# A bias product moved ahead of the first products, and v's bias loaded as columns, in an attention kernel

## The chip, the cores and the metric

The kernel runs on one core of one Trainium2 chip. The metric is the device time of one launch in microseconds. Times here are medians of several runs of the same program; the profile is of one further execution.

## The reference

The inputs are x of shape (4, 64, 64, 256), three weight matrices with their biases, and a factor gamma, all in float32. Each of the four images is self-attention over its 4096 positions:

```
q = x @ Wq + bq            # (B, 64, 64, 128)
k = x @ Wk + bk            # (B, 64, 64, 128)
v = x @ Wv + bv            # (B, 64, 64, 256)
pq, pk, pv = (t.reshape(B, -1, 4096) for t in (q, k, v))
energy = einsum('bcn,bcm->bnm', pq, pk)
attention = softmax(energy, axis=-1)
out = einsum('bcm,bnm->bcn', pv, attention)
return gamma * out.reshape(B, 64, 64, 256) + x
```

## The kernel before

Each product in float32 is made of three products of a shorter type (`F32R`), so every operand is first split into three forms: `h`, an upper part, `l`, the rest, and `d`, the difference of both. ScalarE (ACT) makes `h` (line 154), VectorE (DVE) makes `l` and `d` (L164); from the third x of the first image on, `two=True`, DVE makes only `l` (L157) and GpSimd (POOL) makes `d` (L160). The products of a group run in the order 2, 0, 1 of the forms: form 2, which is `d`, comes first, in a call of its own, and its result is then scaled in place and gets its bias before forms 0 and 1 are added to it in PSUM.

The order of all instructions is written out by hand (`manual_schedule`): each engine runs its own instructions in the order of the program's text, and waits for others by semaphores. DMAs are issued from the queues of SP (`nc.sync`), ACT (`nc.scalar`) and POOL (`nc.gpsimd`).

The prologue is what the change touches. It loads the weights (`raw`), the biases bq, bk and bv as rows on one partition (`rows`), and the first pieces of x (`xs4`, four slots of 128 x 512 numbers; there are `NI` = 16 pieces to an image). It keeps TensorE (PE) busy with `warm(n)`, n products of a matrix of ones that nobody reads (L139). `weights(0)` and `weights(1)` make the forms of the weights of q and k together and of v: ACT `h` (L173), DVE or POOL a scaled copy (L171), DVE `d` and `l` (L175, L177). These and the forms of x are generators: each `next` emits one step.

For each piece i of x the first image then does:

- `transposed` (L215): four transposes on PE, into one of two PSUM banks; `x_forms` (L154 to L164);
- `products(0, i, 0, (2,))` and `(0, 1)`: q and k, four and eight matmuls (L240), with `seed_qk` between them, in which DVE scales what is there and adds `bias` (L251);
- `qk_forms`: ACT (L269) and DVE twice (L272), and their stores by SP (L293);
- `products(0, i, 1, (2,))` and `(0, 1)`: v, likewise, with `seed_v` between them, in which ACT scales and adds `bvs`, a column for each half (L258 twice); `v_forms`.

The accumulators of these products take turns over four PSUM banks, so the third x's first products need the bank that `qk_forms` of the first x reads.

`bias` has bq and bk on every partition: a product of a row of ones and `rows` spreads them (L591), and ACT scales the result (L592). `bvs` has bv as two columns; two products with one column each turn the row bv (L610), and ACT scales them (L617). Both are made in the prologue and used for all images. `ident`, the identity that the transposes need, is made by POOL, and `gam` is loaded through POOL's queue (L142) and scaled twice (L602, L603).

After the 16 pieces the main loop goes over the images, in each over 8 groups of 512 positions and, for each group, 16 pairs of blocks of 128: energy products (L322, L337), exponentials (L340), their forms and sums on ACT and DVE, and the products with v (L394), with the next image's projections spread among them.

Of the kernel before, what the change touches and what calls it, by code (L numbers as in the profile page):

```python
# [20 lines left out]
def kernel(  # L21
# [36 lines left out]
    nc = tc.nc  # L58
# [42 lines left out]
    with ExitStack() as fast:  # L101
# [22 lines left out]
        nc.scalar.dma_start(raw[:, 0, :, C2:], wk.rearrange("(k p) d -> p k d", p=P))  # L124
        nc.sync.dma_start(raw[:, 1], wv.rearrange("(k p) e -> p k e", p=P))
        nc.gpsimd.memset(zs, 1.0)
        rows = work.tile([P, 2, XB], F32, tag="xin", name="rows", bufs=1)[:1]
        rows = rows.rearrange("p s f -> p (s f)")
        make_identity(nc, ident)
        nc.vector.tensor_scalar(ones_r, zs.to_broadcast([P, P]), 1.0, None, ALU.mult)  # L130
        nc.scalar.dma_start(rows[:, :C2], bq.unsqueeze(0))
        nc.scalar.dma_start(rows[:, C2:C], bk.unsqueeze(0))
        nc.scalar.dma_start(rows[:, C:], bv.unsqueeze(0))
        nc.scalar.activation(zs, zs, AF.Exp)
        wp = ps_e.tile([P, P], F32, tag="e", name="wp")

        def warm(times):
            for _ in range(times):
                nc.tensor.matmul(wp, ones, ones, start=True, stop=True)  # L139
# [70 lines left out]
        def transposed(b, i):  # L210
            xs = loads.pop(("x", b, i))
            tp = units["xt", b, i] = bank(f"xt_{b}_{i}", [P, KC, 2, P], b, 0)
            for k in range(KC):
                for s in range(2):
                    nc.tensor.transpose(tp[:, k, s, :], xs[:, s, k * P : (k + 1) * P], ident)  # L215
# [11 lines left out]
        def products(b, i, w, fs):  # L227

            xf = units["xf", b, i]
            if fs[0] == 2:  # L230
                units[w, b, i] = bank(f"qv{w}_{b}_{i}", [P, 2, C], b, 1)
            to = units[w, b, i]
            for s in range(2):
                for f in fs:
                    for k in range(KC):
                        if w:
                            left, right = wf[:, 1, f, k, s * P : (s + 1) * P], xf[:, f, k]
                        else:
                            left, right = xf[:, f, k, s, :], wf[:, 0, f, k]
                        nc.tensor.matmul(  # L240
                            to[:, s, :],
                            left,
                            right.rearrange("p s a -> p (s a)") if w else right,
                            start=(f == 2 and s == k == 0),
                            stop=(f == 1 and k == KC - 1),
                            skip_group_check=True,
                        )
# [337 lines left out]
        next(x0)  # L585
        next(x0)
        next(w0)
        next(w1)
        products(0, 0, 0, (2,))
        bb = ps_e.tile([P, KC + C], F32, tag="e", name="bb")  # L590
        nc.tensor.matmul(bb[:, KC:], ones[:1], rows[:, :C], start=True, stop=True)  # L591
        nc.scalar.activation(bias, bb[:, KC:], AF.Identity, scale=REST)  # L592
        seed_qk(0, 0)
        transposed(0, 1)
        load_x(0, 4)
        x1 = x_forms(0, 1)
        next(x1)
# [6 lines left out]
        for i in range(NI):  # L604
            products(0, i, 0, (0, 1))
            qk = qk_forms(0, i)
            next(qk)
            if i == 0:
                for eh in range(KC):
                    nc.tensor.matmul(  # L610
                        bb[:, eh : eh + 1],
                        rows[:, C + eh * P : C + (eh + 1) * P],
                        ones[:1, :1],
                        start=True,
                        stop=True,
                    )
                nc.scalar.activation(bvs, bb[:, :KC], AF.Identity, scale=REST / E)  # L617
                products(0, 0, 1, (2,))
                seed_v(0, 0)
                transposed(0, 2)  # L620
                load_x(0, 5)
                x2 = x_forms(0, 2)
                next(x2)
            if i + 1 < NI:
                products(0, i + 1, 0, (2,))
                seed_qk(0, i + 1)
            next(qk)
            next(qk)
            next(qk, None)
            if i == 0:  # L630
                next(x2)
            products(0, i, 1, (0, 1))
            vs = v_forms(0, i)
            next(vs)
            next(vs)
            next(vs, None)
            if i + 1 < NI:
                products(0, i + 1, 1, (2,))
                seed_v(0, i + 1)
            if i + 3 < NI:  # L640
                transposed(0, i + 3)
                for _ in x_forms(0, i + 3):
                    pass
            load_x(0, i + 6)
            store()
            if i in (7, 10):
                cross(i // 9)
            elif i in (8, 11):
                energy(i // 9)
            elif i in (9, 12):  # L650
                upper(i // 10)
            elif i == 14:
                halves(0)
            if 1 <= i <= NJ:
                load_q(0, 0, i - 1)
            if i in (2, 4, 6):
                load_k(i // 2 - 1)
            elif i in (8, 11):
                load_k(3 + i // 9)
# [274 lines left out]
```

## Time and profile before

| what | value |
|---|---|
| time, median of 3 runs | 2359.55 us (2359.01 to 2359.71) |
| profiled execution, its own time | 2358.56 us |
| its span, first to last instruction | 2356.7 us |
| mean granted TensorE clock | 0.997 |
| busy: PE, DVE, ACT, POOL | 2341.8, 2128.1, 1871.1, 389.1 us |
| DMA | 413.69 MB, mean 176 GB/s |

PE, DVE, ACT and POOL are the engines; PEld is PE's weight load, which overlaps its matmuls; SP issues DMAs. A name such as `qv L240` is the tile that is written and the line of the kernel; an arrow in "L251 <- PE qv" names what ended an engine's wait. The profile lists a float32 matmul as several records; a matmul of the shorter type is one. Times within the profile count from its first instruction.

### The profile page before, as it was taken

The page shows a single profiled execution, that of the slowest core. Times are in us where ns is not written, and L with a number is a line of the kernel's source. Part 1 is how long each engine was busy: PE and PEld are TensorE (multiplying, and loading weights), DVE is VectorE, ACT ScalarE, POOL GpSimd, SP SyncE. Part 2 cuts the span into 40 slices and gives each one's busy share as a digit, 9 for nine tenths or more (in the row PEclk, how much of TensorE's full clock was granted, in tenths as well). Part 3 has the DMA queues.
Part 4 walks back from the last instruction along what each step waited for, and adds up shares of the span by engine and source line. Part 5 has one row for each costly group of instructions (what it writes and reads, how often), then busy time and mean ns, then how long its engine had stood idle before and what let it go on. Part 6 is the DMA issues. An engine that isn't in the chain of part 4 may idle for free.

```text
span 2356.7 us, 31990 instructions
## 1 busy us (share of the span) xinstructions
PE 2341.8 (99%) x11110; PEld 1956.9 (83%) x11110; DVE 2128.1 (90%) x2098; ACT 1871.1 (79%) x3075; POOL 389.1 (17%) x665
## 2 busy tenths in 40 slices
PE   9999999999999999999999999999999999999998
PEld 8888888888888888888888888888888888888886
DVE  7989999989999899998999999999989888888888
ACT  6788778888788887888878888778887777888785
POOL 6211111111211111111121111111112111111110
PEclk9999999999999999999999999999999999999999
DMA  8556665556975556555597555665559554444453
GB/s 267 165 162 178 175 175 156 174 150 174 305 241 176 147 174 187 161 159 162 157 344 222 162 165 157 178 173 158 172 152 352 160 134 120 122 130 118 130 130 96
DMA packets 178764, 413.69 MB, mean 176 GB/s; under 512 B 25986, under 2 KB 76421, under 8 KB 178596
## 3 DMA queue, kind: packets, MB, share of 16 engines
q0 software_dynamic: 94144, 280.53, 45.2%
q1 hardware_dynamic: 83902, 130.77, 15.5%
q8 instruction: 91, 1.49, 0.3%
q14 instruction: 77, 0.63, 0.1%
q10 hardware_dynamic: 550, 0.26, 0.0%
HBM read 306.51 MB, written 104.98 MB: 175 GB/s over the span
## 4 chain that ended last, share of the span: by engine, by line
PE 97%; ACT 1%; DVE 1%; issue 0%; DMA 0%; POOL 0%; DVEq 0%; ACTq 0%
PE a L394 39%; PE e L337 20%; PE b L394 19%; PE e L322 10%; PE qv L240 8%; PE xt L215 1%; PE z L432 1%; ACT x L340 0%; ACT o L408 0%; ACT e L323 0%; DVE f L272 0%; DMA xs<-in_x_dram 0%; DVE v L164 0%; ACT h L346 0%; DVE ld L373 0%
## 5 line engine op out<-in xcount | busy, mean ns | idle before, releaser
L340 ACT ACTIVATE x<-e 128x512 f32<-128x512 f32 x960 | 522.3, 596 | 295.5 <-PE e L337 289.2
L357 DVE TENSOR_TENSOR s<-s,x 128x1024 f32<-128x1024 f32 x480 | 587.2, 1223 | 93.4 <-ACT x L340 90.8
L371 DVE TENSOR_TENSOR ld<-x,h 128x1024 fp32r<-128x1024 f32 x480 | 586.8, 1222 | 88.7 <-ACT h L346 57.9
L394 PE MATMUL a<-h,v 128*128 128x512 f32 x2048 | 641.0, 394 | 0.0
L323 ACT ACTIVATE e<-e 128x512 f32<-128x512 f32 x1024 | 546.8, 572 | 108.9 <-PE e L322 108.6
L394 PE MATMUL a<-ld,v 128*128 128x512 f32 x2048 | 632.8, 390 | 0.0
L394 PE MATMUL b<-ld,v 128*128 128x512 f32 x2048 | 631.7, 390 | 0.5 <-DVE ld L373 0.4
L309 POOL DMA_DIRECT2D k<-kf x512 | 272.2, 532 | 1912.2 <-PE e L337 1800.0
L373 DVE SCALAR_TENSOR_TENSOR ld<-h,x 128x1024 fp32r<-128x1024 f32 x480 | 585.5, 1220 | 0.0
L337 PE MATMUL e<-q,k 128*128 128x512 f32 x2048 | 548.9, 390 | 1.1
L346 ACT ACTIVATE h<-x 128x1024 fp32r<-128x1024 f32 x480 | 510.4, 1063 | 13.3
L394 PEld LDWEIGHTS b<-ld,v 128*128 128x128 f32 x2048 | 384.1, 188 | 83.8 <-issue 1.1
L394 PEld LDWEIGHTS a<-ld,v 128*128 128x128 f32 x2048 | 384.4, 188 | 83.1
L337 PEld LDWEIGHTS e<-q,k 128*128 128x128 f32 x2048 | 383.1, 188 | 84.5 <-ACT e L323 6.0
L394 PEld LDWEIGHTS a<-h,v 128*128 128x128 f32 x2048 | 368.6, 189 | 69.4 <-ACT o L408 7.3
L322 PE MATMUL e<-q,k 128*128 128x512 f32 x1024 | 316.0, 390 | 0.0
L322 PEld LDWEIGHTS e<-q,k 128*128 128x128 f32 x1024 | 191.7, 188 | 40.7 <-issue 0.2
L240 PEld LDWEIGHTS qv<-wf,xf 128*128 128x128 f32 x768 | 107.5, 192 | 11.2 <-POOL xf L160 1.1
L240 PE MATMUL qv<-wf,xf 128*128 128x256 f32 x768 | 112.9, 286 | 2.4 <-DVE xf L164 0.9
L240 PEld LDWEIGHTS qv<-xf,wf 128*128 128x128 f32 x768 | 106.7, 192 | 8.4 <-ACT s L433 0.7
L240 PE MATMUL qv<-xf,wf 128*128 128x256 f32 x768 | 110.9, 284 | 0.4 <-ACT s L433 0.3
L272 DVE SCALAR_TENSOR_TENSOR f<-f,qv 128x512 fp32r<-128x512 f32 x128 | 85.9, 682 | 3.4 <-ACT f L269 3.1
(82 smaller groups left out, 1016.5 us busy)
## 6 DMA issues: line engine op xcount, KB each, us to landing
k<-kf POOLq DMA_DIRECT2D x512, 384.0 KB, 3.7
vf<-vf SPq DMA_DIRECT2D x48, 768.0 KB
v<-vf POOLq DMA_DIRECT2D x48, 768.0 KB, 8.1
kf<-f SPq DMA_DIRECT2D x128, 192.0 KB
qd<-f SPq DMA_DIRECT2D x128, 192.0 KB
q<-qd POOLq DMA_DIRECT2D x31, 768.0 KB, 4.7
o<-in_x_dram POOLq DMA_DIRECT2D x31, 512.0 KB, 7.4
out_dram<-o SPq DMA_DIRECT2D x31, 512.0 KB
```

The lines of the kernel that those rows point to most:

```text
L240: nc.tensor.matmul(to[:, s, :], left, right.rearrange("p s a -> p (s a)") if w else right, start=(f == 2 and s == k == 0), stop=(f == 1 an ...
L272: nc.vector.scalar_tensor_tensor(f[:, :, :, j, :], h.bitcast(F32), s, y, ALU.mult, op)
L309: nc.gpsimd.dma_start(t, kf[b, u % NU])
L322: nc.tensor.matmul(e, *forms(n, i, 2), start=True, stop=False, skip_group_check=True)
L323: nc.scalar.mul(e, e, -REST)
L337: nc.tensor.matmul(e, *forms(n, i, f), start=False, stop=(f == 1), skip_group_check=True)
L340: nc.scalar.activation(x[:, i, :], e, AF.Exp, scale=(1.0 + E) ** 3 / E)
L346: nc.scalar.activation(h, units[n], AF.Identity, scale=UPPER)
L357: nc.vector.tensor_tensor(s, s, x, ALU.add)
L371: nc.vector.tensor_tensor(l, x, h.bitcast(F32), ALU.subtract)
L373: nc.vector.scalar_tensor_tensor(d, h.bitcast(F32), 1.0 + E, x, ALU.mult, ALU.subtract)
L394: nc.tensor.matmul(to, vall[:, t, f, i, j * P : (j + 1) * P], units[n][f][:, i, :], start=(t == 0 and i == 0 and f != 1), stop=(t == NU - ...
```

## The change

The change does four things in the prologue.

- The product that spreads bq and bk (L591, now L589) and ACT's scaling of it (L592, now L590) come before `next(w1)` and ahead of the first form-2 products of q and k.
- bv is no longer a part of `rows`. Two DMAs from POOL's queue, issued ahead of the identity, write it straight into the two columns of `bvs`; POOL scales these in place. The two products L610 and ACT's L617 go, and so does the load of bv as a row in ACT's queue.
- One more `warm(1)` follows the transposes of the second x.
- The second step of the third x's forms (`l` on DVE and `d` on POOL) moves from behind `qk_forms` of the first x to right behind the first step.

```diff
         nc.gpsimd.memset(zs, 1.0)
-        rows = work.tile([P, 2, XB], F32, tag="xin", name="rows", bufs=1)[:1]
-        rows = rows.rearrange("p s f -> p (s f)")
+        for eh in range(KC):
+            nc.gpsimd.dma_start(bvs[:, eh : eh + 1], bv[eh * P : (eh + 1) * P].unsqueeze(1))
+        rows = work.tile([P, XB], F32, tag="xin", name="rows", bufs=1)[:1]
         make_identity(nc, ident)
         nc.vector.tensor_scalar(ones_r, zs.to_broadcast([P, P]), 1.0, None, ALU.mult)
         nc.scalar.dma_start(rows[:, :C2], bq.unsqueeze(0))
-        nc.scalar.dma_start(rows[:, C2:C], bk.unsqueeze(0))
-        nc.scalar.dma_start(rows[:, C:], bv.unsqueeze(0))
+        nc.scalar.dma_start(rows[:, C2:], bk.unsqueeze(0))
...
         next(w0)
+        bb = ps_e.tile([P, C], F32, tag="e", name="bb")
+        nc.tensor.matmul(bb, ones[:1], rows, start=True, stop=True)
+        nc.scalar.activation(bias, bb, AF.Identity, scale=REST)
         next(w1)
+        nc.gpsimd.tensor_scalar(bvs, bvs, REST / E, None, ALU.mult)
         products(0, 0, 0, (2,))
-        bb = ps_e.tile([P, KC + C], F32, tag="e", name="bb")
-        nc.tensor.matmul(bb[:, KC:], ones[:1], rows[:, :C], start=True, stop=True)
-        nc.scalar.activation(bias, bb[:, KC:], AF.Identity, scale=REST)
         seed_qk(0, 0)
         transposed(0, 1)
+        warm(1)
         load_x(0, 4)
...
             if i == 0:
-                for eh in range(KC):
-                    nc.tensor.matmul(
-                        bb[:, eh : eh + 1],
-                        rows[:, C + eh * P : C + (eh + 1) * P],
-                        ones[:1, :1],
-                        start=True,
-                        stop=True,
-                    )
-                nc.scalar.activation(bvs, bb[:, :KC], AF.Identity, scale=REST / E)
                 products(0, 0, 1, (2,))
                 seed_v(0, 0)
                 transposed(0, 2)
                 load_x(0, 5)
                 x2 = x_forms(0, 2)
+                next(x2)
                 next(x2)
...
             next(qk, None)
-            if i == 0:
-                next(x2)
             products(0, i, 1, (0, 1))
```

## The prediction

> **What bounds the kernel now.** I read the page first, for what sets the end.
>
> ```profile
> PE 2341.8 (99%) x11110; PEld 1956.9 (83%) x11110; DVE 2128.1 (90%) x2098; ACT 1871.1 (79%) x3075; POOL 389.1 (17%) x665
> ...
> PE 97%; ACT 1%; DVE 1%; issue 0%; DMA 0%; POOL 0%; DVEq 0%; ACTq 0%
> ```
>
> PE is busy for 99% of the span of 2356.7 us and is 97% of the chain that ended last. The change leaves that work alone: it touches only the first 20 us, so all that it can win or lose is there. Next I read the chain in order of time, its beginning:
>
> ```profile
> 7.44 0.64 PE bb L591 x2
> ...
> 8.52 0.71 DVE qv L251
> ...
> 9.28 2.07 PE qv L240 x8
> 11.35 0.94 PE bb L610 x4
> 12.29 1.15 PE qv L240 x4
> 13.44 0.85 PE xt L215 x4
> ...
> 17.75 1.29 POOL xf L160
> ...
> 19.08 2.18 PE qv L240 x16
> ...
> 21.70 2.88 PE qv L240 x24
> ```
>
> Ahead of 19.08 PE alternates with ACT, DVE and POOL: it waits for the bias (ACT's L592 and DVE's L251, 8.10 to 9.28) and for the third x's last form (DVE's L157 and POOL's L160, 17.07 to 19.08). From 19.08 the chain is PE without a gap to about 65 us, in periods of 3.32 us. Last, the table by stretches; after the stretch and its length come the busy times of PE, PEld, DVE, ACT and POOL, then the granted clock:
>
> ```profile
> 5.41:8.83 3.42, 2.40 (x14) 1.50 (x13) 2.68 (x5) 1.67 (x4) 1.91 (x3) 1.00 0.85 286
> 8.83:12.24 3.41, 2.96 (x13) 2.73 (x13) 2.78 (x5) 1.06 (x2) 0.00 (x0) 0.50 0.29 77
> 12.24:15.65 3.41, 3.41 (x17) 3.41 (x17) 0.46 (x1) 1.58 (x4) 0.00 (x0) 0.50 0.00 0
> 15.65:19.07 3.42, 2.59 (x22) 2.38 (x21) 3.31 (x6) 2.43 (x5) 1.32 (x2) 1.00 0.59 201
> ```
>
> ```profile
> 8.00:9.00 1.00, 0.66 (x5) 0.42 (x4) 0.48 (x1) 0.69 (x2) 0.47 (x3) 0.91 0.38 131
> ```
>
> From 8.83 to 15.65 PE runs at half clock: 0.91 over 8 to 9 is half for the last 0.17 us, and the same table has 0.67 for 15 to 16, half for the first 0.65. That is 6.83 us, two stretches of 3.41. A matmul of L240 then takes 0.22 us (0.85 for the four transposes at 13.44) instead of 0.12 (2.88 for 24). PE was 70% busy in the stretch before the clock fell, and 76% in 15.65 to 19.07, after which it stayed.
>
> **The change, part by part.** I follow it to one mark: the start of the first products of the third x, 19.08 now. After it PE is full, so what is won there reaches the end, if DVE keeps up; it does, since in each 3.32 us period its queue waits 0.23 us for ACT (L157 on L154).
>
> *The bias product moved up.* Its rows land at 4.20 and 5.58, and PE is idle from 5.85 to 6.71; the product takes 0.64 and fits there, ending about 6.4. ACT then writes `bias` at 6.4 to 6.8, ahead of its second weight form (L173, 6.49 now), which goes to about 6.7 to 7.3. Behind that stands the second x's first form, due at 7.9: covered. The form's reader, L175 on DVE, needs POOL's `scaled` at 8.06 anyway. L251 now waits only for DVE's own L177, which ends at 7.85, so it runs 7.77 to 8.47 instead of 8.52 to 9.22, and the eight products start at 8.53 instead of 9.28: **0.75 won**. If the rows landed later, the first 0.9 us of that would still cost nothing.
>
> *One warm-up (2 records, 0.22) and the transposes* stand at 7.3 to 8.1, where PE would wait for L251: nothing.
>
> *v's bias by DMA.* The four L610 records and L617 go: 0.94 on PE's path at half clock, **0.94 won** (0.5 at full clock, by half the row). Added are two POOL DMAs and one POOL multiply. The nearest row is the other small POOL load:
>
> ```profile
> 1.49 0.71 POOL L142 DMA_DIRECT2D gam<-in_L_conv_gamma_dram  x1 [0.17 <-issue]
> ```
>
> ```profile
> DMA to landing us min/median/max: 4.8/4.8/4.8
> ```
>
> Two issues at 0.71 push the identity from 1.32 to 2.74; the transposes need it at 4.18, when x lands: 1.4 us of cover. The three loads land at about 5.7, 6.4 and 7.7 by 4.8 each. The multiply (0.22, as L602) stands behind `scaled` on POOL, done at 8.3; ACT needs it at 10.3. Bounds: nothing for a landing up to about 9.9, and one us for each us after that. A gain is excluded, since nothing waits for these but L258. I take nothing, as gam's row has the same number of 4-byte pieces.
>
> *bv's row* leaves ACT's queue (0.28): its table load starts earlier, but ACT then waits for Wk until 4.45 as before: nothing. SP's loads of the third and fourth x go out 0.3 to 0.9 earlier behind Wv in the same queue: nothing, as they are needed at 10 and 12.8.
>
> *The third x's second form moved up.* DVE idles 3.58 us ahead of L251 at 15.19; L157 (0.69) goes into that, and POOL's L160 (1.29) starts behind it instead of after L272. The wait of PE from about 18.1 to 19.08 goes: **about 1.0**. L157 now stands ahead of L251 of the second x and of both L272; L251 ends about 0.2 before PE needs it, so a cost appears only if ACT gives the form more than 0.2 late, at most 0.69. What is late next is L272: the third x's product reuses the bank that L272 reads.
>
> *The clock.* In the changed kernel PE is busy in 5.41 to 8.83 from 5.41 to 6.35, 6.71 to 8.1 and 8.53 to 8.83: 2.63 us, 77%. That is over the 76% that kept the clock and the 70% that lost it. So I take it that the clock is kept. Then, from 8.53: 8 products to 9.58 (0.12 each, 0.1 to start), 4 to 10.05, transposes to 10.49, 4 to 10.96; ACT's two L258 end at 11.18, so PE waits to 11.24 (a new wait of 0.28); 8 and 4 to 12.8, transposes to 13.2, 8 to 14.16; POOL's form is there at 13.8, and L272 ends at 14.19. The mark falls at 14.24 instead of 19.08: **4.84 won**. Of it 0.75 is the bias, 0.94 L610, 1.0 POOL's wait; the rest, 2.1, is the clock net of the new waits. A tenth goes for starts that I didn't see; I take 4.75.
>
> The profiled execution took 2358.56 (span 2356.7 and 1.86 around it), 0.99 under the median of 2359.55. The sum gives 2358.56 - 4.75 = 2353.81, and with that 0.99 **2354.8** for the median.
>
> The clock is where a rule speaks against the change. The Trainium skill, "TensorE: Matmul & The Clock Gate", section "Why this matters for your kernels", asks only that PE has no gap over about 3 us; the longest gap ahead of 8.83 is 0.85 and the clock fell, so the trace differs and the measurement decides.
>
> **The rivals.** *One stretch at half clock.* Counted by matmul time alone (0.12 and 0.11 a record, 0.64 for the bias) the stretch that lost the clock has 2 warm-up records, 4 of L240, the bias and 4 transposes, 1.78 us (52%); in the one that kept it 16 of L240 and 4 transposes begin, 2.36 us (69%); the changed one has 1.78 + 0.22 (warm-up) + 0.30 (from 8.53) = 2.30 (67%): in between. If that is too little, the clock falls at 8.83 and is back at 12.24, PE being full. Then the eight products have some 2.5 records at full clock, and the rest to 12.24 at 0.215: the second x's first products end at 12.5, not 14.95; the mark comes at 15.3, 3.8 won: 2355.75. For it speaks that 87% busy in 8.83 to 12.24 did not bring the clock back.
> The Trainium skill, same page, "Part 4: PE-mode transpose", says transposes don't count as busy in the same way; without their 0.44 the stretches are 39% (lost), 56% (kept) and 54% (changed), the same order, so the trace before can't tell.
>
> *Two stretches at half clock, as before*, if the gate looks at something that the fill doesn't change. Then POOL's wait is hidden either way; PE goes at 0.215 from 8.83 to 15.65 and comes to the mark at 16.8: 2.3 won, 2357.25. Against it: PE would be full from 8.53 on, as in 12.24 to 15.65, which brought it back.
>
> *The gain stops at DVE* between 66 and 75 us, where the chain is DVE's: 2359.5. Against it: DVE's work follows PE's products there and moves with them.
>
> *Slower: v's bias lands late.* ACT's L258 and, on POOL, the third x's form stand behind the landing. If the 4-byte pieces go one by one, at four times gam's 4.8 us, they land at 1.6 + 19.2 = 20.8; L258 ends at 22.0 and the products that follow start there instead of at 14.95; with POOL's wait and the half clock behind that gone, 5.7 are lost: 2365.2. It is slower from a landing of about 15 on. Against it: gam's row.
>
> **How the numbers follow.** Clock kept 0.48; one stretch 0.27; two 0.10; stops at DVE 0.05; late landing 0.05; unforeseen 0.05. 0.2% (4.7 us) is about what a measurement of this kernel can tell from no change; the forecast lies just beyond it. I count three quarters of the forecast's chance and a little of the second case (the runs' half clock can have been longer than the profile's, being 1 us over it) as faster: 0.40. Slower is the late landing and little more: 0.06. The range goes from 2353.7 (kept, and the 0.99 of the median over the profile won too) to 2357.4 (two stretches).
>
> **What would show it.** Right: clock 1.00 in every stretch from 5.41 on; L251's first at 7.8; no L610; no idle PE ahead of the third x's first products, at about 14.3; periods of 3.32 from there. Wrong: 0.50 in any stretch after 8.83 (rivals one and two), a wait of L258 for POOL or a DMA (the slower one), idle PE at L215 before 4.2 grown (identity late), or more idle PE at 66 to 76 than now.

## The result and the profile after

The change took 2354.91 us (median of 22 runs, 2352.77 to 2357.05), the kernel before beside it 2358.92 us (22 runs, 2355.47 to 2360.45): a ratio of 0.9984, 95% interval 0.9978 to 0.9991, so 4.0 us faster by the medians. The forecast was 2354.8. Left out here and below are one run of k_later (2577.58 us) and one of before beside it (2911.9 us), with mean clocks of 0.85 and 0.75. The profiled execution of the change took 2357.05 us (span 2355.3), the longest of its 22, so its first 20 us say more than its total. First the page: PE's busy time, and the shares of the chain that ended last.

```profile
PE 2340.0 (99%) x11108; PEld 1955.6 (83%) x11108; DVE 2127.6 (90%) x2098; ACT 1870.2 (79%) x3074; POOL 391.2 (17%) x668
...
PE 97%; ACT 1%; DVE 1%; issue 1%; DMA 0%; POOL 0%; SPq 0%; ACTq 0%; DVEq 0%; POOLq 0%
```

What bounds the kernel is as before. PE was busy for 2341.8 us then: the 1.8 us less are the two products L610 and the time at half clock, net. The chain of waits in order of time (start, length, what ran) has the prediction's steps one by one:

```profile
6.15 0.64 PE bb L589 x2
...
7.80 0.70 DVE qv L251
...
8.55 1.23 PE qv L240 x8
...
10.80 0.46 ACT qv L258
...
11.30 1.70 PE qv L240 x12
...
14.42 2.14 PE qv L240 x16
```

L251 at 7.80 (forecast 7.77), the eight products at 8.55 (8.53), PE again behind L258 at 11.30 (11.24), and the mark, the third x's first products, at 14.42 (14.24; before 19.08). The bias product ended at 6.79 and not at 6.4, which DVE's L177 ahead of L251 still covered. The table by stretches shows the clock (after the length come the busy times of PE, PEld, DVE, ACT and POOL, the granted clock, the DMA share and GB/s):

```profile
5.41:8.83 3.42, 3.01 (x18) 2.27 (x18) 3.35 (x6) 2.05 (x4) 2.40 (x4) 1.00 0.83 283
8.83:12.24 3.41, 3.25 (x27) 3.05 (x27) 2.49 (x5) 1.94 (x4) 0.33 (x1) 1.00 0.30 88
12.24:15.65 3.41, 3.38 (x29) 3.21 (x28) 3.41 (x7) 2.43 (x5) 1.98 (x2) 1.00 0.37 120
```

27 and 29 matmuls stand in the second and third stretch, where before had 13 and 17 at half clock. The new loads of `bvs` are in the row of their line, which ends with the time to landing:

```profile
L128 POOL DMA_DIRECT2D bvs<-in_L_conv_bv_dram x2: 581/640/699, 1.3 to 2.0; - x2
...
DMA to landing us min/median/max: 3.9/4.1/4.3
```

They landed by 6.3, the multiply ran at 7.8, and L258 at 10.3 waited for neither. Up to the mark 4.66 of the forecast's 4.84 us were won. Past it something appears that the prediction did not have:

```profile
30.94 2.25 issue
33.21 0.56 POOL q L303
...
34.31 1.28 POOL v L160
35.59 1.23 POOL xf L160
...
36.86 3.61 PE qv L240 x16
```

The waits and the table by stretches say what it is:

```profile
ACT f L269 <- DMA qd<-f: 3.6, 2, 3.4
...
POOL q L303 <- DMA qd<-f: 2.7, 2, 2.3
```

```profile
36.70:40.12 3.42, 3.26 (x15) 3.26 (x16) 3.04 (x5) 1.33 (x3) 2.64 (x3) 0.50 1.10 373
```

POOL's queue stood at the load of q (L303) until the store that writes that q to DRAM had landed; the form of x behind it in the queue (L160) came late; PE was idle from 34.56 to 36.86, and the clock fell for one stretch. At the same time a second instruction stood behind the stores: ACT's L269, which writes the buffer that they read, waited 3.4 us until 34.71. The first product with v (L394) starts at 68.91 instead of 69.94: of 4.66 us won at the mark 1.03 were left in this execution. From there on nothing differs: from the first to the last product L394 that writes `a` it is 2277.27 us before and 2277.06 after.

### The profile page after: what moved, and what is told of

The parts are those of the page before. It is cut to its first block, busy times and chain, and to the rows that moved or that the text cites. A ratio compares the mean times of both kernels' runs of the same rounds, so it can differ in the third digit from the quotient of the medians.

```text
span 2355.3 us, 31990 instructions
## 1 busy us (share of the span) xinstructions
PE 2340.0 (99%) x11108; PEld 1955.6 (83%) x11108; DVE 2127.6 (90%) x2098; ACT 1870.2 (79%) x3074; POOL 391.2 (17%) x668
## 4 chain that ended last, share of the span: by engine, by line
PE 97%; ACT 1%; DVE 1%; issue 1%; DMA 0%; POOL 0%; SPq 0%; ACTq 0%; DVEq 0%; POOLq 0%
PE a L394 39%; PE e L337 20%; PE b L394 19%; PE e L322 10%; PE qv L240 7%; PE xt L215 1%; PE z L432 1%; ACT x L340 0%; ACT o L408 0%; ACT e L323 0%; DMA qd<-f 0%; DMA xs<-in_x_dram 0%; POOL v L160 0%; DVE v L164 0%; POOL xf L160 0%
## 5 line engine op out<-in xcount | busy, mean ns | idle before, releaser
L394 PE MATMUL a<-h,v 128*128 128x512 f32 x2048 | 641.0, 394 | 0.0
L394 PE MATMUL a<-ld,v 128*128 128x512 f32 x2048 | 632.8, 390 | 0.0
L394 PE MATMUL b<-ld,v 128*128 128x512 f32 x2048 | 631.8, 390 | 0.5 <-DVE ld L373 0.4
L394 PEld LDWEIGHTS b<-ld,v 128*128 128x128 f32 x2048 | 384.2, 188 | 83.8 <-issue 1.1
L394 PEld LDWEIGHTS a<-ld,v 128*128 128x128 f32 x2048 | 384.5, 188 | 83.0
L394 PEld LDWEIGHTS a<-h,v 128*128 128x128 f32 x2048 | 368.6, 189 | 69.2 <-ACT o L408 7.3
L322 PE MATMUL e<-q,k 128*128 128x512 f32 x1024 | 316.1, 390 | 0.0
L322 PEld LDWEIGHTS e<-q,k 128*128 128x128 f32 x1024 | 191.8, 188 | 40.5
L272 DVE SCALAR_TENSOR_TENSOR f<-f,qv 128x512 fp32r<-128x512 f32 x128 | 85.7, 680 | 5.1 <-ACT f L269 4.9
```

Source lines behind the costliest of these rows:

```text
L272: nc.vector.scalar_tensor_tensor(f[:, :, :, j, :], h.bitcast(F32), s, y, ALU.mult, op)
L322: nc.tensor.matmul(e, *forms(n, i, 2), start=True, stop=False, skip_group_check=True)
L394: nc.tensor.matmul(to, vall[:, t, f, i, j * P : (j + 1) * P], units[n][f][:, i, :], start=(t == 0 and i == 0 and f != 1), stop=(t == NU - ...
```

## The experiments

**Two questions.** What wins the time up to the mark, and what takes part of it back between the mark and L394? On the first, the prediction's theory was separate prices (bias 0.75, L610 0.94, POOL's wait 1.0) and a clock that stays up because PE is busier; the rival is that the clock alone is most of it. On the second, the theory is that the DMA engines are full in 20 to 48 us, so that q, which goes to DRAM and back, can't come earlier; the rival is that one instruction stands in the wrong place in a queue.

The DMA row of the table by stretches, 20 to 48 us, first before, then the run `after_again` of the change:

```profile
20.00:48.00 28.00, 28.00 (x230) 27.45 (x229) 24.67 (x40) 20.70 (x43) 23.59 (x24) 1.00 0.97 305
```

```profile
20.00:48.00 28.00, 26.42 (x218) 25.95 (x217) 23.31 (x38) 20.66 (x43) 23.13 (x24) 1.00 1.07 358
```

The DMA share, the last column but one, was 0.97 already in before (it adds up the time of all packets, so it can pass 1). All runs are in one table; the columns from "profiled" on (the execution's own time, the clock, the mark, idle PE between the mark and 66 us, L394) are of the one profiled execution of each.

| run | median us | lowest to highest | profiled | clock full | mark | idle PE after it, at | first L394 |
|---|---|---|---|---|---|---|---|
| before | 2358.92 | 2355.47 to 2360.45 | 2358.56 | 5.41 to 8.83, from 15.65 | 19.08 | none over 0.2 | 69.94 |
| the change | 2354.91 | 2352.77 to 2357.05 | 2357.05 | 5.98 to 36.70, from 40.12 | 14.42 | 2.3 L160 | 68.91 |
| after_again | 2354.96 | 2353.80 to 2357.60 | 2354.97 | from 4.55 | 14.34 | 1.6 L160 | 66.64 |
| bias_only | 2355.64 | 2354.71 to 2358.04 | 2355.88 | from 6.41 | 15.99 | 0.9 L322 | 67.62 |
| vbias_only | 2356.62 | 2355.32 to 2358.17 | 2356.12 | 4.49 to 7.90, from 11.31 | 16.63 | 0.3 L322 | 67.92 |
| before_fill | 2355.91 | 2355.34 to 2357.13 | 2356.21 | from 6.17 | 16.93 | 0.3 L322 | 67.93 |
| no_fill | 2355.08 | 2354.15 to 2356.54 | 2356.13 | from 13.55 | 16.36 | 0.9 L160 | 67.87 |
| x2_back | 2354.99 | 2353.95 to 2355.51 | 2354.74 | from 6.31 | 15.39 | 0.4 L322 | 66.50 |
| q_late | 2358.56 | 2356.83 to 2360.16 | 2359.12 | 4.75 to 38.88, from 45.71 | 14.34 | 3.0 L322 | 70.70 |
| cross_late | 2354.88 | 2353.57 to 2357.41 | 2355.71 | from 4.87 | 14.27 | 1.9 L160, 0.2 L272 | 67.11 |
| q_cross_late | 2362.27 | 2359.60 to 2365.69 | 2364.77 | 6.06 to 57.26, then with breaks | 14.66 | 3.0 L272, 2.5 L160 | 77.06 |
| no_kstore | 2353.48 | 2353.02 to 2356.64 | 2356.64 | from 13.39 | 16.69 | 0.3 L160 | 68.00 |
| k_later | 2358.88 | 2355.31 to 2361.76 | 2360.36 | 5.48 to 53.26, from 56.68 | 14.78 | 3.8 and 0.4 L322, 0.5 L160 | 72.00 |
| q_direct | 2355.05 | 2354.45 to 2357.91 | 2357.91 | from 13.71 | 16.98 | 1.4 L272 | 69.43 |

Before was run beside each group of experiments and had medians of 2358.55, 2358.21, 2358.30 and 2358.67. The experiments have 11 runs each (k_later 10), and each ratio to before has an interval of some 0.0009 to either side, 2.1 us: differences of one us between two rows are not shown by the medians alone. Nor is the ratio quite that of the two medians (for bias_only 0.9992 against 0.9989), so a gain read from medians can be some 0.8 us too large.

The last column decides the time: the own time of the profiled execution less its L394 is 2288.1 to 2288.6 us in thirteen of the fourteen profiles, and 2287.7 in q_cross_late. So an execution that takes one us less has its L394 one us earlier, to half a us. The "half" clock of no_fill, no_kstore and q_direct ahead of 13.4 us is read from the pace of their matmuls, as the profile's clock records begin only there.

### Which part wins what up to the mark

**bias_only**: before with the bias product early and nothing else.

```diff
         next(w0)
+        bb = ps_e.tile([P, KC + C], F32, tag="e", name="bb")
+        nc.tensor.matmul(bb[:, KC:], ones[:1], rows[:, :C], start=True, stop=True)
+        nc.scalar.activation(bias, bb[:, KC:], AF.Identity, scale=REST)
         next(w1)
         products(0, 0, 0, (2,))
-        bb = ...
```

> Before with the bias product and ACT's scaling of it ahead of next(w1) and the first form-2 products, and no other part of the change. Theory (0.75 us of PE's wait for the bias goes): L251's first at 7.8 where it was 8.52, and the mark 0.4 to 0.75 us earlier than in a run of before with the same clock, so 18.3 with two stretches at half clock; the time 0.4 to 0.75 us under before's. Rival (the shorter wait also keeps the clock, since PE is busier in the stretch that ends at about 8.8): the mark at 16.5 or less and the time 2 us or more under before's.

Measured: 2355.64 us, ratio to before 0.9992 (0.9983 to 1.0001), the mark at 15.99, 3.1 us earlier than in before.

```profile
6.41:9.82 3.41, 2.83 (x18) 2.16 (x18) 3.41 (x7) 1.50 (x3) 1.94 (x3) 1.00 0.56 170
9.82:13.24 3.42, 3.25 (x25) 2.99 (x25) 2.39 (x5) 2.11 (x5) 0.00 (x0) 1.00 0.27 80
```

The rival held, in this execution: with L251 at 7.97 the clock was not lost, though L610 and POOL's wait are still there. By the medians this one edit has two thirds of the gain (2.7 of 4.0 us), though the interval just takes in no change. Of the 3.1 us at the mark the wait for the bias itself is 0.55 (L251 at 7.97, in before 8.52).

**vbias_only**: before with the two DMAs into `bvs`, without L610 and L617, and nothing else (that part of the change).

```diff
+        for eh in range(KC):
+            nc.gpsimd.dma_start(bvs[:, eh : eh + 1], bv[eh * P : (eh + 1) * P].unsqueeze(1))
...
-        nc.scalar.dma_start(rows[:, C:], bv.unsqueeze(0))
...
+        nc.gpsimd.tensor_scalar(bvs, bvs, REST / E, None, ALU.mult)
...
-                for eh in range(KC):
-                    nc.tensor.matmul(bb[:, eh : eh + 1], ...)
-                nc.scalar.activation(bvs, bb[:, :KC], AF.Identity, scale=REST / E)
```

> Before with v's bias as columns by DMA and no other part of the change: the two products L610 and ACT's L617 go. Theory (0.94 us at half clock on PE's path): the mark comes 0.5 to 0.9 us earlier than in a run of before with the same clock, so about 18.2 where two stretches are at half clock, and the time is 0.5 to 0.9 us under before's, with the landing of bvs ahead of 7 us. Rival (POOL's two more DMAs delay the third x's form or the identity): no gain at the mark, and ACT's L258 or PE's L215 waits longer.

Measured: 2356.62 us, ratio 0.9995 (0.9986 to 1.0004, so no change is not excluded), the mark at 16.63. Here the clock did fall, for one stretch instead of two:

```profile
7.90:11.31 3.41, 3.24 (x15) 2.84 (x15) 2.94 (x5) 1.05 (x3) 0.67 (x3) 0.50 0.33 95
```

15 matmuls in 3.41 us. The next stretch has 28 and full clock. So of the 2.45 us at the mark some 0.9 can be L610 and the rest is that the clock came back one stretch earlier. No wait for a landing shows at L258 or L215; the rival fell.

**before_fill**: before with three more warm-ups in the first place and two behind the transposes of the second x.

```diff
-        warm(2)
+        warm(5)
...
         transposed(0, 1)
+        warm(2)
```

> The kernel before with only more products of ones: three more ahead of the first products, two more behind the second x's transposes. Nothing else differs, so only the clock can win. Theory (the gaps cost the clock): granted clock 1.00 from 5.4 us on, and 2.1 us faster than before (worked out with all durations at full clock: the L610 pieces take half, and the wait for POOL's form of the third x eats part). Rival (the gate counts something that products of ones don't give, or closes in any case): half clock between 8.8 and 15.7 us as before, and the time within 0.3 us of before.

Measured: 2355.91 us, ratio 0.9989 (0.9980 to 0.9998), the clock full from 6.17, the mark at 16.93. Work that nobody reads, without any step being made shorter, wins 2.6 us by the medians, and its runs lie within 1.8 us of each other, where before's lie within 5.0. So the rival fell: in this profile warm-ups were enough to keep the clock.

This also shows what the medians compare. Of the 107 runs of before beside the experiments, 31 lie at 2355.3 to 2356.7 us, where ten of before_fill's eleven lie; 28 of these 31 have a mean clock of 0.999. Another 37 lie at 2357.9 to 2359.7 with 0.996 or 0.997; 0.997 is the value of before's profile, in which the clock fell for two stretches. It is likely, though none of the 31 was profiled, that before kept its clock in them. The other 39 (2357.1 to 2360.9, with 0.998 or 0.999) have no profile either. Against the 31 (median 2355.9) the change is one us faster, not four. If the reading is right, most of the 4.0 us is that the clock is lost less often.

**no_fill**: the change without `warm(1)` and without the `warm(2)` that before has too.

```diff
         transposed(0, 0)
-        warm(2)
...
         transposed(0, 1)
-        warm(1)
```

> The change without its added warm(1) and without the warm(2) that before already has ahead of the second weight forms: PE's idle time ahead of 8.5 us grows by about 0.7 us and nothing else moves. Theory (the clock falls where the share of busy time in a stretch of 3.41 us is too small): clock 0.50 for one or two stretches after about 8.5, the mark (third x's first products) at 15.3 to 16.8 instead of 14.3, and the time 1 to 2.5 us over the change's, less what the later waits for q give back. Rival (the fill is not what keeps the clock; the shorter waits for bias and L610 are): clock 1.00 after 8.5, the mark at 14.3, the same time within 0.5 us.

Measured: 2355.08 us, ratio 0.9988 (0.9979 to 0.9997). The profiled execution runs at half clock to 13.55 (the clock did not fall, it came up late) and has its mark at 16.36, 2 us later than the change's, within the theory's range. Its own time is 2356.13, 1.05 over the median of its runs, and its L394 is 1.2 later than after_again's: of the 2.0 us lost at the mark 1.2 reach the end. The median is the change's within 0.2 us, as the rival says; which beginning the other ten runs had is not known. So this run does not settle what the fill is worth in the change.

**x2_back**: the change with the third x's second form where it was.

```diff
                 x2 = x_forms(0, 2)
                 next(x2)
-                next(x2)
...
             next(qk, None)
+            if i == 0:
+                next(x2)
```

> The changed kernel with the third x's second form put back to its old place, behind the first x's L272. Theory: PE waits for POOL's form again ahead of the third x's first products, and since the clock is now full that wait is shorter than the 1.0 us of before: worked out, the products start at about 15.2 instead of 14.4 us, 0.8 us slower than the changed kernel, 4.0 faster than before. Rival (the move does nothing because L272 and the PSUM bank set the start in any case): the same as the changed kernel within 0.3 us.

Measured: 2354.99 us, ratio 0.9987 (0.9978 to 0.9996). The mark comes at 15.39 behind 0.7 us of idle PE, 1.05 later than in after_again, so the move is worth at the mark what was forecast. But L394 starts at 66.50, where after_again has 66.64: at the end it is worth nothing.

**The parts with the clock full.** Four profiles have the full clock from 6.41 us at the latest, and each has one part of the change more than the one ahead of it: before_fill (no part, mark 16.93), bias_only (15.99), x2_back (v's bias and `warm(1)` too, 15.39) and after_again (all, 14.34). The steps are 0.94, 0.60 and 1.05. Of the 0.94 some 0.39 is before_fill's own fill (its L251 is at 8.91, before's at 8.52), which leaves 0.55 for the bias; the 0.60 is L610, whose four records take 0.53 in bias_only. From 19.08 to 14.34 that leaves 2.5 for the clock. So the parts do add, once the clock is counted by itself and the others at full clock. At L394 before and these four read 69.94, 67.93, 67.62, 66.50 and 66.64: the clock brings 2.0 us to the end, the bias 0.3 (0.9 is waited at L322), L610 1.1 and the third x's form nothing. These are single executions.

### Where it goes after the mark

**after_again**: the change itself, to see whether the wait at L303 belongs to it.

> The changed kernel once more, unaltered, for a second profile. Theory: the first products of the third x start at about 14.4 us with the clock at 1.00 until then, as in the first profile; what differs between executions comes later, between 20 and 40 us, where PE in the first profile waited 2.3 us for POOL (L160) and then ran one stretch of 3.41 us at half clock. If that loss is an accident of one execution, this profile lacks it, the second period mark (the fifth x's transposes) and the end both come about 4.7 us ahead of before, and the median is some 4 to 5 us under before's. Rival: the wait for POOL belongs to the change, because everything comes earlier and the loads of q now wait for the stores of q; then it is here again, with 2 to 3.5 us lost, and the profile's span is about 2355.

Measured: 2354.96 us, ratio 0.9988 (0.9979 to 0.9997). The waits of PE and POOL between the mark and 66 us (in all, times, longest):

```profile
PE qv L240 <- POOL xf L160: 1.6, 1, 1.6
```

```profile
POOL q L303 <- DMA qd<-f: 1.7, 1, 1.7
```

The wait belongs to the change, as the rival says, though it costs less than the rival's 2 to 3.5 us; the stretch at half clock behind it does not come each time. Mark to L394 takes 52.30 us here and 50.86 in before: of 4.74 us won at the mark 3.30 reach L394, and 1.4 are given back.

**q_late**: the four loads of q one x later, so that POOL does not wait for their stores.

```diff
-            if 1 <= i <= NJ:
-                load_q(0, 0, i - 1)
+            if 2 <= i <= NJ + 1:
+                load_q(0, 0, i - 2)
```

> The changed kernel with each of the four loads of q into SBUF issued one x later (after x 2 to 5, not 1 to 4), so that POOL meets a store that has had one more period of 3.3 us to land. Theory (POOL's queue waits for the landing of q's stores, and the forms on POOL behind it come late for PE): the wait goes, PE has no idle time and full clock between 15 and 60 us, and the median is 0.5 to 3 us under the changed kernel's. Rival (the wait is the DMA engines' load, whatever waits for it): the same as the changed kernel within 0.5 us, with the idle time moved to another instruction.

Measured: 2358.56 us, ratio 1.0002 (0.9993 to 1.0011): all of the gain gone.

```profile
PE e L322 <- DMA q<-qd: 3.0, 1, 3.0
```

POOL's wait went and PE's came: the last load of q, issued at 33.99, landed at 39.80, and the first energy product needed it at 36.81. Two stretches at half clock followed (38.88 to 45.71). So there is a second reader that is just in time: in before, that load landed at 41.57 and L322 began at 41.73.

**cross_late**: the change with L322 and what follows it one x later.

```diff
-            if i in (7, 10):
+            if i in (8, 11):
                 cross(i // 9)
-            elif i in (8, 11):
-                energy(i // 9)
             elif i in (9, 12):
-                upper(i // 10)
+                energy(i // 10)
+            elif i in (10, 13):
+                upper(i // 11)
```

> The change, and the first energy products (L322) with what follows them one x later. After's last quarter of q lands at 37.7 to 39.8 us, and L322 now would be due about 41.5. Theory (there are two waits in the stretch of full DMA queues: POOL's queue behind the q load L303, and L322 behind q's landing): the first stays, 1.6 to 2.3 us of idle PE at about 34.5, so the first product with v (L394) starts at 66.5 to 69 as in the change, and the time is within 0.7 us of the change's (about 2354.9). Rival (only L322's need counts, POOL's wait is an accident of one execution): no idle PE over 0.5 us after the mark, L394 at about 65.2, the time 1.5 us under the change's.

Measured: 2354.88 us, ratio 0.9988 (0.9979 to 0.9997).

```profile
PE qv L240 <- POOL xf L160: 1.9, 1, 1.9
PE qv L240 <- DVE f L272: 0.2, 1, 0.2
```

The theory held: giving the second reader time leaves the first wait as it was.

**q_cross_late**: both, q's loads one x later and L322 two x later.

```diff
-            if i in (7, 10):
-                cross(i // 9)
+            if i in (9, 12):
+                cross(i // 10)
...
-            if 1 <= i <= NJ:
-                load_q(0, 0, i - 1)
+            if 2 <= i <= NJ + 1:
+                load_q(0, 0, i - 2)
```

> The change, the q loads (L303) one x later, and the energy products (L322) two x later. Theory: POOL's wait for the store ahead of L303 goes, since that store is a whole x older, and L322's wait goes too, so PE is full from 14.3 to the first product with v, which starts at about 65.3; the time is 1.3 us under the change's (about 2353.6). Rival (what the DMA engines move in 20 to 48 us binds, whichever instruction happens to wait): idle PE of 1.5 us or more shows at another line in 30 to 50 us and the time stays within 0.5 us of the change's.

Measured: 2362.27 us, ratio 1.0019 (1.0010 to 1.0028): 4 us slower than before by the medians, and 8.7 us from what the theory said.

```profile
PE qv L240 <- DVE f L272: 3.0, 3, 1.7
```

With both readers out of the way PE waits first at 31.44 to 33.17 for L272. That stands behind ACT's L269, which waited 2.9 us, until 31.11, for a store of q to land: both write the buffer that the stores read. That is the rival: another instruction waits. The rest of the loss is later (2.5 us at 53.19 and two stretches at half clock), where the late energy steps meet the main loop's beginning; what of it is order and what is DMA was not taken apart.

**no_kstore**: the change without a part of the bytes. The stores of k's second half are left out for the first eight x, and the blocks that they would have filled are written in the main loop from other k tiles, so this kernel is for timing alone.

```diff
-                stores.append((kf[b, i // 2 + NU // 2 * s][:, i % 2], f[:, s, 1]))
+                if b or i > 7 or s == 0:
+                    stores.append((kf[b, i // 2 + NU // 2 * s][:, i % 2], f[:, s, 1]))
...
+            if n < 4:
+                nc.sync.dma_start(kf[0, n + 8], loads["k", n + 2].bitcast(F32))
```

> The change without the stores of k's second half (L293, 196 KB each) of the first eight x, 1.57 MB of the some 10.8 MB that the DMA engines move in 20 to 48 us; so that nothing unwritten is read, four of k's blocks of the first image are written in the main loop's first steps from other k tiles (their values are wrong). The same instructions of PE, DVE, ACT and POOL ahead of the main loop. Theory (the bytes that are moved in 20 to 48 us bind, and the waits of POOL's q load L303, of L322 and of L272 are where it shows): landings of the stores stay under 3 us, no idle PE over 0.4 us in 20 to 50 us, the first product with v (L394) at about 65.3 (14.3 and the 50.9 us that before takes from the mark), the time 1.3 us under the change's, about 2353.6. Rival (the order of the queues binds, not the bytes): POOL's L303 still waits 1.5 us or more for its store, L394 at 66.5 or later, the same time within 0.5 us.

Measured: 2353.48 us, ratio 0.9984 (0.9974 to 0.9993). 7 of its 11 runs lie at or under 2353.6 us, and 4 of the 33 of the change (its own 22 and after_again's 11). That is the time that the theory forecast (about 2353.6). The profiled execution, though, is the longest one (2356.64), with the clock at half to 13.39:

```profile
PE qv L240 <- POOL xf L160: 0.3, 1, 0.3
```

```profile
6.57:9.98 3.41, 3.41 (x14) 2.76 (x15) 2.53 (x5) 1.33 (x3) 1.82 (x4) 1.00 0.47 162
9.98:13.39 3.41, 3.41 (x18) 3.41 (x18) 1.97 (x4) 1.54 (x4) 0.00 (x0) 1.00 0.25 77
13.39:16.80 3.41, 3.41 (x29) 3.26 (x29) 2.74 (x5) 2.52 (x7) 1.29 (x1) 1.00 0.24 77
```

14, 18 and 29 matmuls: half clock in the first two, whatever the clock column says. With its mark at 16.69 this execution can't show what an early mark would meet. The nearest to it is no_fill, with all stores and the mark at 16.36: PE waits 0.9 us there, 0.3 here, and POOL's queue stands at the load of q for 1.2 and 0.6. Landings as short as the theory asked for (under 3 us) do not show: the four loads of q took 3.8 to 6.3 us, and the DMA share for 20 to 48 us is still 1.04 (9.1 MB, where the change moved 9.5 and before 8.5, not the 10.8 of the expectation). That fewer bytes let the gain through rests on the times.

**k_later**: k's second and third loads at the ninth and eleventh x instead of the fifth and seventh, and the next two behind them.

```diff
-            if i in (2, 4, 6):
-                load_k(i // 2 - 1)
-            elif i in (8, 11):
-                load_k(3 + i // 9)
+            if i == 2:
+                load_k(0)
+            elif i in (8, 10, 12, 14):
+                load_k(i // 2 - 3)
```

> The change with k's loads L309 for the second and third pair of blocks at the ninth and eleventh x instead of the fifth and seventh, and the next two behind them: 0.79 MB leave the stretch before 40 us and come after it. Theory (bytes bind): POOL's wait for the store ahead of L303 and the idle PE at about 34.5 shrink from 1.6 to 2.3 us to under 1, L394 at 65.5 to 66.2, the time 0.5 to 1 us under the change's (about 2354.2). Rival (only what is moved ahead of the q stores themselves counts, and those k loads stand behind L303): the idle PE stays at 1.5 us or more and the time is the same within 0.5 us.

Measured: 2358.88 us, ratio 1.0005 (0.9995 to 1.0014).

```profile
PE e L322 <- DMA k<-kf: 3.8, 1, 3.8
PE qv L240 <- POOL xf L160: 0.5, 1, 0.5
```

The second line is the theory's: with 0.79 MB out of the way ahead of 40 us the wait at L160 is 0.5 instead of 1.6 to 2.3. The first is a price that neither theory had: the load for the second pair of blocks, issued at 45.65, lands at 53.76, when PE has stood 3.8 us, and the clock falls at 53.26. The time forecast failed.

**q_direct**: q's first four pieces by SP into the tile that L322 reads, without DRAM; POOL's L303 goes.

```diff
-                stores.append((qd[b, i // NJ + NG // 2 * s][:, i % NJ], f[:, s, 0]))
+                if b == s == 0 and i < NJ:
+                    stores.append((loads["q", 0, 0][:, i].bitcast(F32), f[:, s, 0]))
+                else:
+                    stores.append((qd[b, i // NJ + NG // 2 * s][:, i % NJ], f[:, s, 0]))
...
-            if 1 <= i <= NJ:
-                load_q(0, 0, i - 1)
```

> The change, with the first group's four q pieces sent by SP straight into the tile that L322 reads, instead of to DRAM and back: POOL's four q loads L303 go, and 0.79 MB of DMA. Theory (what is won at the mark is lost to q, which comes back too late from DRAM): no wait of POOL for a store of q and no idle PE over 0.4 us in 20 to 50 us, the last q piece landed by 38; where the clock rises before 7 us the mark is at 14.3 and the first product with v (L394) at about 65.3, the time 2353.0 to 2353.6; where it rises only at about 13.4 the mark is 16.7 and the time some 2 us more; the median about 2353.6, 1.3 us under the change's. Rival (the bytes of the other stores and loads still bind): idle PE of 1 us or more at L160, L272 or L322 in 30 to 50 us, and the time within 0.5 us of the change's (2354.9).

Measured: 2355.05 us, ratio 0.9985 (0.9976 to 0.9994), the change's time.

```profile
PE qv L240 <- DVE f L272: 1.4, 1, 1.4
```

The rival held. No wait for q is left and 0.79 MB less are moved, and PE waits at L272, with a mark that is late anyway (16.98). Ahead of L272 stands ACT's L269 again, at 33.10. The profile puts its wait of 2.5 us down to PE's transposes, whose result it does not read; a store that still reads the buffer is likelier, but not shown here. So q's way through DRAM is one place where the stretch is short of time, and not the only one.

**What stands.** Shown at the mark: the clock, the bias, L610 and the third x's form have the prices above, and warm-ups alone keep the clock. Shown after it: the waits move from L303 to L322 to L272 as one reader after another is freed (q_late, q_cross_late, q_direct), and moving L322 alone (cross_late) or making the mark earlier by the x2 move (x2_back) changes nothing at the end. Supported by run times only: fewer stores let most runs reach the time that the mark promises (no_kstore). Open: whether it is the bytes as such and how many have to go, since 1.57 MB of stores helped and 0.79 MB of q loads did not, and no run had fewer bytes and an early mark in its profile. No variant with all of its work in it was faster than the change.

## Why the prediction was right, and where it was wrong

- **The bound and the place**: right. From L394 on both kernels take the same time to 0.2 us, so the rival that ends the gain at DVE in 66 to 75 us fell as well.
- **The bias product, 0.75**: right. L251 at 7.80 and the products at 8.55, to 0.03 us. The row of bk was later than reckoned in some executions (after_again, cross_late and q_direct have PE wait 0.2 to 0.3 us for it), which the prediction's 0.9 us of cover took up in the first two.
- **v's bias by DMA, nothing on POOL and 0.94 on PE**: right on POOL, and too much on PE. The 0.94 is L610 at half clock, in a sum that keeps the clock; at full clock it is worth 0.60 at the mark. The mark itself was worked out step by step at full clock, so only the split is off, and "the rest, 2.1" for the clock is some 2.5. The issues took 0.70 and 0.58 us, the identity was done at 3.14, long ahead of x, and the landings (5.1 and 6.3) were earlier than the 5.7 and 6.4 forecast. The slower rival, the late landing, has nothing for it.
- **The third x's second form, 1.0 at the mark**: right as a price (1.05 by x2_back), without effect on the time.
- **The clock**: kept in the profiled execution, as forecast, and worth what the prediction left for it and a little more. But it is not won by the sum of the edits: bias_only keeps it alone, before_fill keeps it with warm-ups alone, and each of them has about 2.7 us by the medians. Where the prediction had prices of 0.75 and 0.94 for two edits, either one alone moved the mark by 2.5 to 3.1.
- **A case that it did not have**: nine profiled executions have the change's beginning up to L258 (the change, after_again, x2_back, q_late, cross_late, q_cross_late, k_later, no_kstore, q_direct). In seven the clock was full by 6.31 at the latest; in two it was half until 13.39 and 13.71, and the mark came at 16.69 and 16.98. That is the second rival's mark (16.8) by another way: the clock did not fall, it came up late.
- **The step that failed**: "After it PE is full, so what is won there reaches the end, if DVE keeps up". DVE kept up; the stores and loads of q and k, in a stretch where the DMA engines are full, did not. 1.4 us (after_again) to 3.6 us (the change's profile, with the half-clock stretch) were given back between the mark and L394. The profile of before had the signs: a DMA share of 0.97 for 20 to 48 us, the last piece of q landed at 41.57, 0.16 us ahead of its first reader, and POOL's queue already stood for stores of q (the waits of before, 19 to 66 us):

```profile
POOL k L309 <- DMA qd<-f: 2.0, 1, 2.0
POOL q L303 <- DMA qd<-f: 0.2, 1, 0.2
```

The prediction looked in that stretch for idle time of PE and found none, but not for how little slack its cover had.
- **The number**: the forecast gain was 4.75 on a median of 2359.55, and 4.0 was measured on one of 2358.92. The gain was 0.74 too high and the base 0.63 too high; that the sum came out within 0.11 us is partly these two against each other, so partly luck. More luck is in it: the base is a median over runs of before that differ by up to 5 us, and much of the gain on it is the clock.
- **The rules on the clock**: the Trainium skill, "TensorE: Matmul & The Clock Gate", section "Why this matters for your kernels", asks for no gap of PE over some 3 us. The change's profile has a second case against it: PE idle for 2.3 us (34.56 to 36.86), and clock 0.50 from 36.70. The Trainium skill, same page, "Part 4: PE-mode transpose", has transposes not count as busy in the same way; the two stretches 6.57 to 9.98 and 9.98 to 13.39 of no_kstore both have four transposes, and the clock rose only behind the second, so transposes alone do not decide it.

## What to carry to other kernels

An early gain is worth what the next shared resource lets through: before carrying it to the end, look in the stages that follow for transfers that land just ahead of their reader, and at the DMA share there, even where PE has no idle time yet. In a stage whose clock can fall, price the clock by itself and the edits at full clock, and try the cheapest edit alone: here one moved product, or warm-ups that nobody reads, had two thirds of the gain by the medians. Look at the spread of the runs too: where over a quarter of them already have the time that the edit is to bring, the median says how often something happens as much as what it costs. And when a wait is removed in a full stretch, expect the next one in line (here L303, L322, then L272) rather than the gain; the one run that came through the stretch had fewer bytes to store.

## What the runs showed of the hardware

- The clock changes at the ends of stretches of 3.41 us, and where these lie differs from execution to execution. In the profiles here it was full from 4.49, 4.55, 4.75, 4.87, 5.41, 5.48, 5.98, 6.06, 6.17, 6.31 or 6.41 us, and in three executions only from 13.39, 13.55 or 13.71. The Trainium skill, "TensorE: Matmul & The Clock Gate", Part 1, has a window of 3413 ns that runs freely and does not start with the kernel; these rows agree. The beginning mattered: in the eleven profiles with an early rise it came at 6.41 us or before; in the other three a stretch ended at 6.57, 6.72 or 6.89, and the rise came two stretches later. In the two of these that have the change's beginning up to L258 (no_kstore, q_direct) the mark is at 16.69 and 16.98, where the others have 14.27 to 14.78 (x2_back 15.39). That the ends of the stretches decide this is a reading; it was not tried.
- At half clock, a stretch in which the profile has PE busy all the time did not bring the clock back (6.57 to 9.98 in no_kstore: 3.41 us busy, but 14 matmuls where the next stretch has 18), and one with 3.24 us and 15 matmuls did (7.90 to 11.31 in vbias_only). The first begins with products of one row; whether these count was not tried.
- With the DMA engines full (a share of 1.07 to 1.09 for 28 to 38 us), the loads of q (L303, 192 KB) that were issued between 27 and 36 us took 5.4 to 6.6 us to land in before and the change; the first one in before, issued at 24.91, took 3.6. A load of k (384 KB) issued at 45.65 in k_later took 8.1.
- The two loads of `bvs`, 128 pieces of 4 bytes each, took 3.9 and 4.3 us to land in the change.
